# Gated cross-attention and mixture of experts: the query weights centred once, raw tokens turned, the inverse deviation as a scale of the exponentials

## The chip, the cores and the metric

One core of a Trainium2 chip runs the whole kernel. The metric is the device time in microseconds; each value is the median of several runs. A single execution is also recorded by the hardware profiler, and all rows of the profile come from that one execution. The engines are named as in the profile: PE is TensorE (PEld its weight loads), DVE is VectorE, ACT is ScalarE, POOL is GpSimd, SP is SyncE, which here only issues DMAs.

## The reference

The input `x` has 32 sequences of 128 tokens with 128 features. A second input, `ctx_512`, has 32 sequences of 128 rows with 64 features. Everything is fp32.

```
h  = layernorm(x)                        # no learned scale: (x - mean) / sqrt(var + 1e-5)
qh = (h @ Wq), kh = (ctx @ Wk), vh = (ctx @ Wv)     # 16 heads of 64
a  = softmax(qh kh^T / 8)                # per head, 128 tokens x 128 rows
x  = x + tanh(g_xattn) * ((a vh) @ Wo + bo)
h2 = layernorm(x)
x  = x + tanh(g_ffn) * (routed experts(h2) + shared expert(h2))
```

The expert part takes sigmoid scores of 32 experts in 4 groups, keeps 2 groups and then 8 experts for each token. The change does not touch it.

## The kernel before, in words

The kernel has two stages: the attention, block by block (one block `b` is one of the 32 sequences, 128 tokens), and then the experts. The first ends and the second begins at about 280 to 310 us.

**Weights folded once.** The kernel never forms keys or values. For each pair of heads it multiplies the query and key weights into one matrix (`products_a` on PE from `wqT_sb` and `wkT_sb`, and `make_a`, which copies the product to `a_sb` and multiplies it by 1/8). `make_c` does the same for values and output weights. Both work in halves of four head pairs, as there are two PSUM tiles `s_ps[0]` and `s_ps[1]`.

**One block.** `layernorm_stats` (L244, L245, DVE) gives mean and variance of a token. `inverse` adds epsilon (L299, DVE) and raises to the power -0.5 (L301, POOL) for four blocks at a time. `normalize` (L307, DVE) writes normalised tokens `xn` for two blocks. `turn_tokens` (L319, PE) transposes them and `tokens_out` (L323, ACT) copies them to `xnT`. `project` (L328, PE) multiplies by `a_sb`, `queries` (L363, ACT) copies out `qT`. `scores(b, g)` (L369, PE) multiplies one half `g` of the heads with the context `kvT_sb` into `s_ps[g]`. `negmax` (L376, DVE) takes the negated maximum of each head's row. `exponentials` (L389, ACT) runs one exponential for each of the eight heads of the half, with that maximum as a bias of one value per partition, and sums the row as it goes (the accumulator is read by a second instruction at the same line). `scaled` takes the reciprocal of the sums (L396, DVE) and multiplies the exponentials by it (L398, POOL). `turned` (L404, DVE) transposes 32 by 32 parts, `weighted` (L415, PE) multiplies with the context, `sums_out` (L424) copies the result out, half on DVE and half on ACT. `attention_out` (L436, PE) multiplies by the folded output weights, and `residual` (L442, DVE) adds the result to `x_all`, in which `add_bias` (L314, POOL) has put the output's bias.

**Order.** Everything stands in an order written out by hand (`tc.manual_schedule()`): each engine runs its own instructions in program order, and semaphores make one engine wait for another. A prelude handles blocks 0 and 1; then the loop over `b` (from L924) works on several blocks at once: in the step of `b` PE computes scores of `b` and `b+1`, the weighted sums of `b-2`, the output of `b-3` and the projection of `b+2`. Every fourth step also has logits (L487, PE; L499, ACT). From block 20 on, `gap` puts small pieces of the experts' routing between them on DVE.

**Loads.** DMAs are issued in program order on the queue of the engine that issues them. At the start ACT's queue takes the two halves of `wqT`; SP's takes `load_x(0)`, `wkT` whole, `load_x(1)`, `load_kvT(0, TB)`, `load_kv(0)`, and then the other weights. `load_rows` issues four small loads on POOL's queue.

Of the kernel before, what the change touches and what calls it, by code (L numbers as in the profile page):

```python
# [17 lines left out]
P = 128  # L18
B = 32
D = 128  # L20
KV = 64
NP = 8
TB = 4
NT = B // TB
TT = TB * P
HP = NP // 2
# [6 lines left out]
ATT_SCALE = 64.0 ** -0.5  # L33
# [21 lines left out]
def gated_cross_attention_moe(  # L55
# [22 lines left out]
    nc = tc.nc  # L78

    const = ctx.enter_context(tc.tile_pool(name="const", bufs=1))  # L80
# [3 lines left out]
    x_all = keep.tile([P, B, D], F32, tag="x", name="x_all")  # L84
# [9 lines left out]
    a2 = attn.enter_context(tc.tile_pool(name="a2", bufs=2))  # L94
    a3 = attn.enter_context(tc.tile_pool(name="a3", bufs=3))
# [31 lines left out]
    def weights(at, w):  # L127
        return x2T[:, NP * at : NP * (at + w)].rearrange("p (h c) -> p h c", h=NP)

    wqT_sb = weights(0, D)  # L130
    wkT_sb = weights(D, KV)
    wvT_sb = weights(D + KV, KV)
    wo_sb = weights(D + 2 * KV, D)
    for half in range(2):
        nc.scalar.dma_start(
            out=wqT_sb[:, half * HP : (half + 1) * HP], in_=wqT[:, half * HP : (half + 1) * HP]
        )
    load_x(0)
    nc.sync.dma_start(out=wkT_sb, in_=wkT)
    load_x(1)  # L140
    load_kvT(0, TB)
    load_kv(0)
    nc.sync.dma_start(out=wvT_sb, in_=wvT)
    nc.sync.dma_start(out=wo_sb, in_=wo)
# [42 lines left out]
    ident = const.tile([P, P], F32, tag="ident", name="ident")  # L187
# [67 lines left out]
    c_sb = aw.tile([P, NP, D], F32, tag="c", name="c_sb")  # L255

    def products_a(half):
        pa = s_ps[half].rearrange("p j q (h k) -> p j (q h) k", k=KV)
        for q in range(HP):
            for j in range(2):  # L260
                r = slice(j * KV, (j + 1) * KV)
                p = half * HP + q
                nc.tensor.matmul(
                    pa[:, j, q, :], wqT_sb[r, p, :], wkT_sb[r, p, :], start=True, stop=True
                )

    def make_a(half):
        pa = s_ps[half].rearrange("p j q (h k) -> p j (q h) k", k=KV)
        for j in range(2):
            nc.vector.tensor_scalar(  # L270
                a_sb[:, half * HP : (half + 1) * HP, j, :], pa[:, j, 0:HP, :], ATT_SCALE, None, ALU.mult
            )

    def make_c(half):
        pc = [o_ps[0][:, j].rearrange("p (h d) -> p h d", d=D) for j in range(2)]
# [15 lines left out]

    v = nc.vector
    mv1 = aw.tile([P, B, 2], F32, tag="mv1", name="mv1")
    xns, xnT, qT, nmax, es, sums, eTs, oTs = ({} for _ in range(8))
    rstds = {}

    def inverse(t):
        ve = a2.tile([P, TB], F32, tag="ve", name=f"ve_{t}")
        v.tensor_scalar(ve, mv1[:, t * TB : (t + 1) * TB, 1], EPS, None, ALU.add)  # L299
        rstds[t] = a2.tile([P, TB], F32, tag="rstd", name=f"rstd_{t}")  # L300
        nc.gpsimd.tensor_tensor(rstds[t], ve, mhalf, ALU.pow)  # L301

    def normalize(p):
        xns[p] = a2.tile([P, 2, D], F32, tag="xn", name=f"xn_{p}")
        for k in range(2):
            c = 2 * p + k
            v.tensor_scalar(  # L307
                xns[p][:, k, :], x_all[:, c, :], mv1[:, c, 0:1], rstds[c // TB][:, c % TB : c % TB + 1],
                ALU.subtract, ALU.mult,
            )  # L310

    def add_bias(p):
        a = x_all[:, 2 * p : 2 * p + 2, :]
        nc.gpsimd.tensor_tensor(a, a, tgbo.unsqueeze(1).to_broadcast([P, 2, D]), ALU.add)  # L314

    def turn_tokens(p):
        xn = xns.pop(p)
        for k in range(2):
            nc.tensor.transpose(o_ps[0][:, 1, k * P : (k + 1) * P], xn[:, k, :], ident)  # L319

    def tokens_out(p):
        xnT[p] = a3.tile([P, 2 * P], F32, tag="xnT", name=f"xnT_{p}")
        nc.scalar.copy(xnT[p], o_ps[0][:, 1, 0 : 2 * P])  # L323

    def project(b):
        x_ = xnT[b // 2][:, b % 2 * P : (b % 2 + 1) * P]
        for p in range(NP):
            nc.tensor.matmul(  # L328
                o_ps[1][:, p // HP, p % HP * P : (p % HP + 1) * P],
                a_sb[:, p].rearrange("d j k -> d (j k)"), x_, start=True, stop=True,  # L330
            )

    def first_place(k):
        return s_ps[1][:, 0, 0, :] if k else o_ps[0][:, 1, 0:P]

    def first_turned(k):

        nc.tensor.transpose(first_place(k), xns[0][:, k, :], ident)

    def first_tokens(k):  # L340
        if k == 0:
            xnT[0] = a3.tile([P, 2 * P], F32, tag="xnT", name="xnT_0")
        nc.scalar.copy(xnT[0][:, k * P : (k + 1) * P], first_place(k))

    def first_projections(b, g):

        for q in range(HP):
            nc.tensor.matmul(
                o_ps[1 - g][:, 0, q * P : (q + 1) * P],
                a_sb[:, g * HP + q].rearrange("d j k -> d (j k)"), xnT[0][:, b * P : (b + 1) * P],  # L350
                start=True, stop=True,
            )
# [21 lines left out]
    def negmax(b, g):  # L374
        nmax[b, g] = a4.tile([P, NP], F32, tag="nmax", name=f"nmax_{b}_{g}")
        v.tensor_reduce(  # L376
            nmax[b, g], s_ps[g].rearrange("p j q k -> p (j q) k"), AX.X, ALU.max, negate=True
        )

    def exponentials(b, g, js=(0, 1)):  # L380
        if (g, js[0]) == (0, 0):
            es[b] = ae.tile([P, 2, 2, HP, P], F32, tag="e", name=f"e_{b}")
        n = nmax[b, g]
        if js[0] == 0:
            sums[b, g] = a4.tile([P, NP], F32, tag="ssum", name=f"ssum_{b}_{g}")
        for j in js:
            for q in range(HP):
                c = slice(j * HP + q, j * HP + q + 1)
                nc.scalar.activation(  # L389
                    es[b][:, g, j, q, :], s_ps[g][:, j, q, :], AF.Exp,  # L390
                    bias=n[:, c], accum_out=sums[b, g][:, c],
                )

    def scaled(b, g):
# [57 lines left out]
    def clear(t):  # L452
# [7 lines left out]
        out=xs[NC * REG :, :].rearrange("(k p) w -> p k w", p=P),  # L460
        in_=zero[:, 0:RW].unsqueeze(1).to_broadcast([P, TAIL // P, RW]),
# [620 lines left out]
    xbs, wrows, wbs, wcs, own, xTs, groups, hs, hTs, ys, idx = ({} for _ in range(11))  # L1082
# [167 lines left out]
    with tc.manual_schedule():  # L1250
# [153 lines left out]
```

## Time and profile before

| | |
|---|---|
| median of 3 runs | 548.38 us (547.67 to 548.81) |
| the profiled execution, its own time | 551.0 us |
| its span, first to last instruction | 549.2 us |
| mean granted PE clock | 0.984 |
| first exponential | 16.45 us |
| start of the copy of the queries (L363), blocks 2 and 31 | 27.88 and 273.75 us |

A row of a group of instructions gives the line, the engine, the operation, output and inputs by name, shapes and count; then, after the bar, busy time in us and mean ns of one; after the next bar the idle time of the engine just before them and who ended it. A row of a wait gives who waited for whom: us in total, how often, the longest. A row of the timeline gives start, duration, engine, line, operation. Instructions of one engine overlap a little, so that a duration is longer than the time from one start to the next; both are used below, and named. A row of a stretch of time gives its length, and busy us and instructions of each engine.

### The profile page before, as it was taken

Reading aid. Unit: us, or ns where it says so; the run is one execution under the profiler, and the core shown is the slowest. Engines: PE = TensorE matmul, PEld = TensorE weight load, DVE = VectorE, ACT = ScalarE, POOL = GpSimd, SP = SyncE. Lnnn points to the kernel's source line nnn. Section 1 sums busy time; section 2 is a strip of 40 time slices with the busy share of each in tenths; the row PEclk is TensorE's granted clock in tenths of the full one; section 3 lists DMA queues with packets and bytes.
Section 4 is the critical chain, followed back from the end, with each engine's and each line's share of the span. In section 5 each row is a group of like instructions: output and inputs, shape, how many; then the busy total and the mean of one; then the engine's idle time right before and its main releaser. Section 6 shows DMA issues by size and latency. Waiting matters only on the chain.

```text
span 549.2 us, 15741 instructions
## 1 busy us (share of the span) xinstructions
PE 514.8 (94%) x5857; PEld 440.9 (80%) x5857; DVE 406.1 (74%) x920; ACT 374.5 (68%) x1407; POOL 276.8 (50%) x248
## 2 busy tenths in 40 slices
PE   5889999999999999998999789999999999999992
PEld 4777888988989988897876556666676799999992
DVE  3779999898898998998887588898644445555551
ACT  1688989989899888997883144444444677777760
POOL 5255557665675756874754641652672212232332
PEclk9899999999999999999999989999999999999997
DMA  8994440805304010000000232131123255453631
GB/s 237 236 331 144 129 174 3 300 4 175 127 20 152 3 42 1 2 2 3 2 2 26 77 94 63 35 72 15 38 49 82 56 118 122 95 131 89 128 88 15
DMA packets 49563, 47.81 MB, mean 87 GB/s; under 512 B 20752, under 2 KB 38848, under 8 KB 49104
## 3 DMA queue, kind: packets, MB, share of 16 engines
q1 hardware_dynamic: 43008, 41.71, 26.6%
q0 software_dynamic: 6192, 4.56, 5.7%
q8 instruction: 48, 0.79, 0.6%
q10 hardware_dynamic: 288, 0.52, 0.4%
q14 instruction: 27, 0.22, 0.2%
HBM read 25.44 MB, written 21.54 MB: 86 GB/s over the span
## 4 chain that ended last, share of the span: by engine, by line
PE 71%; DVE 20%; POOL 2%; ACT 2%; issue 1%; DMA 1%; another core or an unknown queue 1%; POOLq 0%; DVEq 0%
PE y L1206 11%; PE o_ps L436 8%; PE s_ps L369 8%; PE o_ps L415 7%; PE u L1190 6%; PE g L1190 6%; PE o_ps L328 6%; PE g L1124 6%; PE u L1126 5%; DVE nmax L376 5%; DVE eT L404 5%; PE ph L1144 3%; DVE xn L307 3%; DVE oT L424 1%; ACT e L389 1%
## 5 line engine op out<-in xcount | busy, mean ns | idle before, releaser
L389 ACT ACTIVATE e<-s_ps,nmax 128x128 f32<-128x128 f32 x512 | 181.6, 384 | 9.7 <-DVE nmax L376 8.3
L398 POOL TENSOR_TENSOR e<-e,rs 128x1024 f32<-128x1024 f32 x64 | 121.4, 1898 | 92.6 <-DVE rs L396 92.6
L1217 POOL DMA_INDIRECT out_dram<-o,idx x35 | 55.1, 1575 | 128.0 <-ACT o L1215 74.9
L389 ACT ACTIVATION_READ_ACCUMULATOR e<-s_ps,nmax 128x1 f32 x512 | 114.0, 223 | 0.0
L376 DVE TENSOR_REDUCE nmax<-s_ps 128x8 f32<-128x1024 f32 x64 | 77.0, 1202 | 11.7 <-PE s_ps L369 11.5
L404 DVE STREAM_TRANSPOSE eT<-e 128x1024 f32<-128x1024 f32 x64 | 78.7, 1229 | 0.9 <-POOL e L398 0.9
L369 PE MATMUL s_ps<-kvT_sb,qT 64*128 64x128 f32 x1024 | 76.0, 289 | 3.0 <-ACT e L389 1.9
L369 PEld LDWEIGHTS s_ps<-kvT_sb,qT 64*128 64x128 f32 x1024 | 63.7, 191 | 18.7 <-issue 11.1
L436 PE MATMUL o_ps<-c_sb,oT 128*128 128x128 f32 x512 | 65.4, 281 | 6.8 <-DVE oT L424 6.8
L436 PEld LDWEIGHTS o_ps<-c_sb,oT 128*128 128x128 f32 x512 | 59.7, 191 | 13.4 <-DVE oT L424 10.5
L415 PE MATMUL o_ps<-eT,kv 32*64 32x256 f32 x2048 | 66.0, 380 | 2.1 <-DVE c_sb L285 1.0
L328 PE MATMUL o_ps<-xnT,a_sb 128*128 128x128 f32 x480 | 59.9, 278 | 0.0
L1196 DVE TENSOR_TENSOR uw<-u,wb 128x512 f32<-128x512 f32 x36 | 24.9, 692 | 46.4 <-PE u L1190 41.5
L328 PEld LDWEIGHTS o_ps<-xnT,a_sb 128*128 128x128 f32 x480 | 56.7, 194 | 0.3 <-issue 0.2
L415 PEld LDWEIGHTS o_ps<-eT,kv 32*64 32x64 f32 x2048 | 49.4, 131 | 8.1 <-DVE c_sb L285 1.4
L1206 PEld LDWEIGHTS y<-ed_sb,hT 128*128 128x128 f32 x272 | 35.5, 191 | 16.0 <-issue 14.3
L698 POOL DMA_INDIRECT xs<-rows,posi x32 | 34.5, 1078 | 19.7 <-DVE nbi L727 11.0
L1131 DVE TENSOR_TENSOR uw<-u,xb 128x512 f32<-128x512 f32 x34 | 23.3, 686 | 24.2 <-PE u L1126 22.5
L1146 ACT COPY hT<-ph 128x512 f32<-128x512 f32 x34 | 19.9, 586 | 27.1 <-PE ph L1144 20.0
L1190 PE MATMUL g<-xT,wc 128*128 128x128 f32 x288 | 38.0, 275 | 0.0
L1190 PE MATMUL u<-xT,wc 128*128 128x128 f32 x288 | 38.0, 275 | 0.0
L1206 PE MATMUL y<-ed_sb,h 128*128 x288 | 37.8, 275 | 0.0
(203 smaller groups left out, 891.2 us busy)
## 6 DMA issues: line engine op xcount, KB each, us to landing
xs<-zero SPq DMA_DIRECT2D x8, 1740.0 KB, 12.2
wb<-wr SPq DMA_DIRECT2D x36, 256.0 KB, 4.0
kv<-in_kv_dram SPq DMA_DIRECT2D x32, 128.0 KB, 3.1
xb<-xs SPq DMA_DIRECT2D x35, 72.5 KB, 2.2
x_all<-in_x_dram SPq DMA_DIRECT2D x8, 256.0 KB
kvT_sb<-in_kvT_dram SPq DMA_DIRECT2D x6, 256.0 KB, 5.5
eg_sb<-in_exp_gT_dram SPq DMA_DIRECT2D x1, 1024.0 KB, 6.2
eu_sb<-in_exp_uT_dram SPq DMA_DIRECT2D x1, 1024.0 KB
```

Of the source, the lines that this page charges most:

```text
L328: nc.tensor.matmul(o_ps[1][:, p // HP, p % HP * P : (p % HP + 1) * P], a_sb[:, p].rearrange("d j k -> d (j k)"), x_, start=True, stop=True,)
L369: nc.tensor.matmul(s_ps[g][:, j, q, :], qT[b][r, g * HP + q, :], kvT_sb[r, b * P : (b + 1) * P], start=True, stop=True,)
L376: v.tensor_reduce(nmax[b, g], s_ps[g].rearrange("p j q k -> p (j q) k"), AX.X, ALU.max, negate=True)
L389: nc.scalar.activation(es[b][:, g, j, q, :], s_ps[g][:, j, q, :], AF.Exp, bias=n[:, c], accum_out=sums[b, g][:, c],)
L398: nc.gpsimd.tensor_tensor(e, e, rs.unsqueeze(2).to_broadcast([P, NP, P]), ALU.mult)
L404: v.transpose(eTs[b][:, g].rearrange("p j q n -> p (j q n)"), es[b][:, g].rearrange("p j q n -> p (j q n)"))
L415: nc.tensor.matmul(o_ps[a // 2][j * KV : (j + 1) * KV, a % 2, 0 : NP * Q].rearrange("k (g q n) -> k g q n", g=2, q=HP), kv_sb[b // TB][r, ...
L436: nc.tensor.matmul(o_ps[0][:, 0, 0:D], o[:, p].rearrange("k a n -> k (a n)"), c_sb[:, p, :], start=(p == 0), stop=(p == NP - 1),)
L698: w = nc.gpsimd.indirect_dma_start(out=xs[:, :], out_offset=bass.IndirectOffsetOnAxis(ap=posi[:, i : i + 1], axis=0), in_=rows[:, first[k] ...
L1190: nc.tensor.matmul(pt[:, q, :], w[:, k, q * P : (q + 1) * P], xTs[j], start=True, stop=True)
L1206: nc.tensor.matmul(ys[j], hT[:, q, :], ed_all[:, bass.ds(groups[j][s] * FG + q * D, D)], start=(s == 0 and q == 0), stop=(s == 1 and q == ...
L1217: w = nc.gpsimd.indirect_dma_start(out=out_rows, out_offset=bass.IndirectOffsetOnAxis(ap=idx.pop(j), axis=0), in_=o, in_offset=None, bound ...
```

## The change

- `wqT_sb` is centred in place, half by half: from each row of 128 query weights its mean is subtracted (`centre`, two DVE instructions a half). Multiplying raw tokens by centred weights is the same as multiplying centred tokens by raw weights, so the mean of a token is no longer subtracted.
- `normalize` and `xn` are gone. PE turns the raw tokens out of `x_all` (`turn_tokens`, `first_turned`); the copies are called `xT`.
- The inverse deviation of a token is applied to its scores: `exponentials` passes `deviation(b)`, one value per partition, as `scale`; `negmax` multiplies the maxima of a half by it, in place (128 partitions x 8 values, DVE). The tiles of `rstd` get three buffers instead of two.
- `make_a` is split: the first head of each pair is copied by DVE, the second by ACT.
- Loads: `wkT` comes in two halves on SP's queue, the first ahead of `load_x(0)`; `load_kvT(0, TB)` goes ahead of `load_x(1)`.
- Prelude: `load_rows` and eight transposes of the identity (`warm`) come first; then centring, the turns of blocks 0 and 1, both halves of the products; the statistics of blocks 0 to 3 come after those, and both halves of the first projections of block 0 before its scores. The statistics of blocks 4 to 8 move to the end of the prelude.

```diff
     for half in range(2):
-        nc.scalar.dma_start(
-            out=wqT_sb[:, half * HP : (half + 1) * HP], in_=wqT[:, half * HP : (half + 1) * HP]
-        )
-    load_x(0)
-    nc.sync.dma_start(out=wkT_sb, in_=wkT)
+        hs_ = slice(half * HP, (half + 1) * HP)
+        nc.scalar.dma_start(out=wqT_sb[:, hs_], in_=wqT[:, hs_])
+        nc.sync.dma_start(out=wkT_sb[:, hs_], in_=wkT[:, hs_])
+        if half == 0:
+            load_x(0)
+    load_kvT(0, TB)
     load_x(1)
-    load_kvT(0, TB)
     load_kv(0)
...
+    def centre(half):
+        hs_ = slice(half * HP, (half + 1) * HP)
+        w = wqT_sb[:, hs_, :]
+        nc.vector.tensor_reduce(mean[:, hs_], w, AX.X, ALU.add)
+        nc.vector.scalar_tensor_tensor(
+            out=w, in0=mean[:, hs_].unsqueeze(2).to_broadcast([P, HP, D]), scalar=-1.0 / D, in1=w,
+            op0=ALU.mult, op1=ALU.add,
+        )
+
+    def warm(n):
+        for _ in range(n):
+            nc.tensor.transpose(o_ps[1][:, 1, 0:P], ident, ident)
...
     def make_a(half):
         pa = s_ps[half].rearrange("p j q (h k) -> p j (q h) k", k=KV)
-        for j in range(2):
-            nc.vector.tensor_scalar(
-                a_sb[:, half * HP : (half + 1) * HP, j, :], pa[:, j, 0:HP, :], ATT_SCALE, None, ALU.mult
-            )
+        a = a_sb[:, half * HP : (half + 1) * HP]
+        w = nc.vector.tensor_scalar(a[:, :, 0, :], pa[:, 0, 0:HP, :], ATT_SCALE, None, ALU.mult)
+        tc.add_to_no_dep_group(f"a{half}", w.ins)
+        w = nc.scalar.mul(a[:, :, 1, :], pa[:, 1, 0:HP, :], ATT_SCALE)
+        tc.declare_no_dep(w.ins, group=f"a{half}", reason="each head of a pair has columns of its own")
...
-    def normalize(p):
-        xns[p] = a2.tile([P, 2, D], F32, tag="xn", name=f"xn_{p}")
-        for k in range(2):
-            c = 2 * p + k
-            v.tensor_scalar(
-                xns[p][:, k, :], x_all[:, c, :], mv1[:, c, 0:1], rstds[c // TB][:, c % TB : c % TB + 1],
-                ALU.subtract, ALU.mult,
-            )
+    def deviation(c):
+        return rstds[c // TB][:, c % TB : c % TB + 1]
...
     def turn_tokens(p):
-        xn = xns.pop(p)
         for k in range(2):
-            nc.tensor.transpose(o_ps[0][:, 1, k * P : (k + 1) * P], xn[:, k, :], ident)
+            nc.tensor.transpose(o_ps[0][:, 1, k * P : (k + 1) * P], x_all[:, 2 * p + k, :], ident)
...
+        v.tensor_scalar(nmax[b, g], nmax[b, g], deviation(b), None, ALU.mult)
...
                 nc.scalar.activation(
                     es[b][:, g, j, q, :], s_ps[g][:, j, q, :], AF.Exp,
-                    bias=n[:, c], accum_out=sums[b, g][:, c],
+                    bias=n[:, c], scale=deviation(b), accum_out=sums[b, g][:, c],
                 )
...
     with tc.manual_schedule():
-        for c in range(TB):
-            layernorm_stats(x_all, mv1, c)
-        inverse(0)
         load_rows()
-        products_a(0)
-        normalize(0)
-        make_a(0)
+        warm(8)
+        for half in range(2):
+            centre(half)
         for k in range(2):
             first_turned(k)
         for k in range(2):
             first_tokens(k)
+        products_a(0)
+        make_a(0)
+        products_a(1)
+        for c in range(TB):
+            layernorm_stats(x_all, mv1, c)
+        inverse(0)
+        make_a(1)
         first_projections(0, 0)
         first_queries(0, 0, nc.scalar.copy)
-        products_a(1)
-        for c in range(TB, 2 * TB):
-            layernorm_stats(x_all, mv1, c)
-        inverse(1)
-        make_a(1)
+        first_projections(0, 1)
+        first_queries(0, 1, v.tensor_copy)
         scores(0, 0)
         negmax(0, 0)
-        normalize(1)
-        first_projections(0, 1)
-        first_queries(0, 1, v.tensor_copy)
...
         queries(2)
-        layernorm_stats(x_all, mv1, 2 * TB)
-        normalize(2)
+        for c in range(TB, 2 * TB + 1):
+            layernorm_stats(x_all, mv1, c)
+        inverse(1)
...
-            if b % 2 == 0 and b + 4 < B:
-                normalize(b // 2 + 2)
```

More of the change, by code (lines that the diff above doesn't have):

```diff
@@ L255, in gated_cross_attention_moe @@
     c_sb = aw.tile([P, NP, D], F32, tag="c", name="c_sb")
+    mean = const.tile([P, NP], F32, tag="mean", name="mean")
+    def centre(half):
[9 more added lines that the diff above has]
+            nc.tensor.transpose(o_ps[1][:, 1, 0:P], ident, ident)
     def products_a(half):
@@ L293, in gated_cross_attention_moe @@
     mv1 = aw.tile([P, B, 2], F32, tag="mv1", name="mv1")
-    xns, xnT, qT, nmax, es, sums, eTs, oTs = ({} for _ in range(8))
+    xT, qT, nmax, es, sums, eTs, oTs = ({} for _ in range(7))
     rstds = {}
@@ L299, in inverse @@
         v.tensor_scalar(ve, mv1[:, t * TB : (t + 1) * TB, 1], EPS, None, ALU.add)
-        rstds[t] = a2.tile([P, TB], F32, tag="rstd", name=f"rstd_{t}")
+        rstds[t] = a3.tile([P, TB], F32, tag="rstd", name=f"rstd_{t}")
         nc.gpsimd.tensor_tensor(rstds[t], ve, mhalf, ALU.pow)
-    def normalize(p):
-        xns[p] = a2.tile([P, 2, D], F32, tag="xn", name=f"xn_{p}")
-        for k in range(2):
-            c = 2 * p + k
-            v.tensor_scalar(
-                xns[p][:, k, :], x_all[:, c, :], mv1[:, c, 0:1], rstds[c // TB][:, c % TB : c % TB + 1],
-                ALU.subtract, ALU.mult,
-            )
+    def deviation(c):
+        return rstds[c // TB][:, c % TB : c % TB + 1]
     def add_bias(p):
@@ L316, in turn_tokens @@
     def turn_tokens(p):
-        xn = xns.pop(p)
         for k in range(2):
-            nc.tensor.transpose(o_ps[0][:, 1, k * P : (k + 1) * P], xn[:, k, :], ident)
+            nc.tensor.transpose(o_ps[0][:, 1, k * P : (k + 1) * P], x_all[:, 2 * p + k, :], ident)
     def tokens_out(p):
-        xnT[p] = a3.tile([P, 2 * P], F32, tag="xnT", name=f"xnT_{p}")
-        nc.scalar.copy(xnT[p], o_ps[0][:, 1, 0 : 2 * P])
+        xT[p] = a3.tile([P, 2 * P], F32, tag="xT", name=f"xT_{p}")
+        nc.scalar.copy(xT[p], o_ps[0][:, 1, 0 : 2 * P])
     def project(b):
-        x_ = xnT[b // 2][:, b % 2 * P : (b % 2 + 1) * P]
+        x_ = xT[b // 2][:, b % 2 * P : (b % 2 + 1) * P]
         for p in range(NP):
@@ L336, in first_turned @@
     def first_turned(k):
-        nc.tensor.transpose(first_place(k), xns[0][:, k, :], ident)
+        nc.tensor.transpose(first_place(k), x_all[:, k, :], ident)
     def first_tokens(k):
         if k == 0:
-            xnT[0] = a3.tile([P, 2 * P], F32, tag="xnT", name="xnT_0")
-        nc.scalar.copy(xnT[0][:, k * P : (k + 1) * P], first_place(k))
+            xT[0] = a3.tile([P, 2 * P], F32, tag="xT", name="xT_0")
+        nc.scalar.copy(xT[0][:, k * P : (k + 1) * P], first_place(k))
     def first_projections(b, g):
@@ L349, in first_projections @@
                 o_ps[1 - g][:, 0, q * P : (q + 1) * P],
-                a_sb[:, g * HP + q].rearrange("d j k -> d (j k)"), xnT[0][:, b * P : (b + 1) * P],
+                a_sb[:, g * HP + q].rearrange("d j k -> d (j k)"), xT[0][:, b * P : (b + 1) * P],
                 start=True, stop=True,
```

## The prediction

> **What bounds the kernel now.** I read the page first, then the busy time of single token blocks, then the waits, then the timeline of ScalarE (ACT) and VectorE (DVE).
>
> ```profile
> span 549.2 us, 15741 instructions
> PE 514.8 (94%) x5857; PEld 440.9 (80%) x5857; DVE 406.1 (74%) x920; ACT 374.5 (68%) x1407; POOL 276.8 (50%) x248
> ...
> PE 71%; DVE 20%; POOL 2%; ACT 2%; issue 1%; DMA 1%; another core or an unknown queue 1%; POOLq 0%; DVEq 0%
> ```
>
> TensorE (PE) carries 71% of the chain, ACT 2%. ACT's 68% is an average over stages, though. The change lies in the attention, so I cut that stage at the copies of the queries (L363, one per block; starts read off the timeline):
>
> ```profile
> core 0: us, PE busy (x) PEld busy (x) DVE busy (x) ACT busy (x) POOL busy (x), PEclk, DMA share, GB/s
> 83.91:92.05 8.14, 8.14 (x132) 7.39 (x132) 7.36 (x14) 7.46 (x35) 6.24 (x6) 1.00 0.01 3
> 92.05:100.19 8.14, 8.14 (x132) 7.39 (x133) 7.75 (x15) 7.46 (x37) 6.12 (x6) 1.00 0.51 149
> 100.19:108.32 8.13, 8.13 (x132) 7.38 (x132) 6.77 (x13) 7.45 (x36) 3.79 (x3) 1.00 0.98 354
> 108.32:117.63 9.31, 9.10 (x140) 8.28 (x140) 8.38 (x17) 7.78 (x37) 6.33 (x6) 1.00 0.02 7
> ```
>
> A step is 8.14 us, PE busy throughout; each fourth step also has logits and takes 9.3. ACT is busy 7.46 of the 8.14, so it has little to give. Its only regular wait is for PE:
>
> ```profile
> ACT oT L424 <- PE o_ps L415: 17.6, 26, 0.7
> ...
> PE o_ps L436 <- DVE oT L424: 6.8, 12, 1.4
> ```
>
> That is 0.68 us a step. PE in turn loses 6.8 us in the whole loop (47 to 274 us) to DVE: all that a lighter DVE could return there.
>
> **The exponentials: the part that decides.** Each of the 512 (L389) gets a second per-partition operand, the inverse deviation as scale beside the maximum as bias; nothing is removed from ACT in the loop. The trace has an exponential with none (L499) ahead of those with one (L389), same 128x128 shape:
>
> ```profile
> 116.04 0.28 ACT L499 ACTIVATE sc<-o_ps 128x128 f32<-128x128 f32 x1
> 116.21 0.37 ACT L389 ACTIVATE e<-s_ps,nmax 128x128 f32<-128x128 f32 x1
> 116.46 0.21 ACT L389 ACTIVATION_READ_ACCUMULATOR e<-s_ps,nmax 128x1 f32 x1
> 116.55 0.38 ACT L389 ACTIVATE e<-s_ps,nmax 128x128 f32<-128x128 f32 x1
> ...
> L1215 ACT ACTIVATE o<-y,tg 128x128 f32<-128x128 f32 x35 | 12.8, 364 | 21.4 <-PE y L1206 17.6 <-PE g L1124 2.5 <-PE u L1126 1.2
> ...
> L1118 ACT COPY xT<-px 128x128 f32<-128x128 f32 x14 | 3.8, 271 | 0.0
> ```
>
> From start to start, one without an operand holds ACT for 0.17 us, one with a bias for 0.25 (116.21 to 116.46): 80 ns for one operand. A scale operand (L1215) against a plain copy (L1118) is 364 - 271 = 93 ns. No row has two. Bounds: nothing, if both are fetched together; 93 ns, if in turn. The rule is in the Trainium skill, "ScalarE: Activation LUTs", section "What ACT_TABLE_LOAD costs": each pointer operand adds about 93 ns. It speaks against this change. By the rule a step gets 16 x 93 = 1.49 us, by start-to-start 16 x 81 = 1.30. I take 87 ns, 1.39 us: the two single-operand rows agree, and one instruction fetching two at once has no row.
>
> ACT per step now, start to start: 16 x 0.343 (0.25 and 0.093 for the accumulator) = 5.49; queries 0.91; oT 0.48; tokens or turned rows 0.27; logits 0.17/4 = 0.04: 7.19. After: 7.19 + 1.39 = 8.58, above PE's 8.14. PE cannot run ahead, since `scores(b+1, 0)` needs the bank that the exponentials read. Handing over in both directions costs some 0.15 us, so ACT decides from a step of about 8.3 on, (8.3 - 7.19)/16 = 69 ns an operand. Summed over the steps between L363 starts:
> - 27.9 to 83.9: the step of b = 1 has 12 exponentials, +1.0; the six after it average 8.33, but one is 8.65 already: +1.6.
> - 83.9 to 229.1: twelve of 8.14 go to 8.58, +5.3; the long ones (9.3, 10.3) have room, 0.
> - 229.1 to 273.8: 8.47, 8.39, 8.02 go to 8.58, +0.9; 10.47 and 9.26 keep theirs.
> - Last blocks: 28 exponentials x 0.087 = 2.4, of which ACT's idle time there (0.66 + 0.19 + 0.35) hides 1.2: +1.2.
>
> Together +10.0 (with 81 ns +8, with 93 ns +12).
>
> **DVE: normalisation out, 64 small products in.** Removed: `normalize`, 32 instructions of 693 ns, 20.9 us busy, one pair per two blocks. Added: 64 products of 128x8 behind `negmax`, 0.12 to 0.17 us each by L299's small form (128x4): about 9 us. But such an instruction can wait for POOL:
>
> ```profile
> 49.40 1.90 POOL L398 TENSOR_TENSOR e<-e,rs 128x1024 f32<-128x1024 f32 x1 [0.51 <-DVE rs L396]
> 50.39 0.93 DVE L299 TENSOR_SCALAR ve<-mv 128x4 f32<-128x4 f32 x1
> ...
> 117.17 0.14 DVE L299 TENSOR_SCALAR ve<-mv 128x4 f32<-128x4 f32 x1
> ```
>
> The same instruction takes 0.14 us alone and 0.93 beside L398: it ends when POOL does. Rule: "GPSIMD Engine Reference", "Specifications", shares SBUF interfaces with VectorE and names contention with its 2-port modes. "VectorE: DVE Perf Modes", "The perf-mode tier table", gives tensor_scalar on fp32 in SBUF such a mode; the product is one. Counting by elements, 64 cost 9 us; by the row, the half-0 ones behind `scaled` meet L398 (1.90 us, started about when L376's 1.2 us does), 32 x 0.7 more = 22 us. Sum -20.9 + 9 + 22 = +10 DVE us, or 0.3 a step. That fits: in the step from 96.2 DVE idles 1.26 us. Queued behind the product are the transpose eT, on which `weighted` waits, and ACT's next exponentials, which come 4 us later. On the path: 0 now that ACT decides; a gain of up to 6.8 us if it didn't.
>
> **The start.** Before, the chain was: x landed 4.90, statistics, inverse (POOL 1.05), normalise, 16 slow products, first exponential at 16.45. After: x behind 128 KB of wk, about 5.1; centring is a reduction of 512 (half of 1.2) and an update of 512 (0.74 at L845), 1.3 a half. With wq's halves at about 3.8 and 5.3 it ends at 5.1 and 6.6. PE at its slow rate: turns 0.5, products_a 2 x 2.0, first projections 2 x 2.0 (L348 x8 at 9.38 took 2.05), scores 2.0, from 5.1: 15.6; maximum and product 1.4: exponential at 17.0, +0.5. At the full rate throughout, the same list takes half, but waits at 9.2 for a_sb's second half behind the four statistics: 12.8, -3.6. Before, PE ran from 6.3 and had its full clock only at about 16. I take it from 13: -0.7, range -3.6 to +0.6. Work hidden: `warm` (8 turns, 2 us in PE's idle first 5 us; if the identity came late, 1 us at most), make_a shared with ACT (idle), rows' DMAs earlier on POOL, one more issue on SP (0.5 us), kvT before x(1), which is read at b = 1. Stats of x(1) move behind queries(2): 5 x 0.4 us of DVE, inside b = 1's slack, at worst 1 us.
>
> **Sum.** 549.2 + 10.0 - 0.7 = 558.5 us of span. That execution's own time was 551.0, so 560.3; its sibling runs have a median of 548.38, to which the same +9.3 gives 557.7.
>
> **Rivals.**
> - Operands fetched together (ends on the other side): ACT stays at 7.19 and PE at 8.14. The start gives 0.7 to 3.6, about half of the 6.8 us wait comes back, so -5: 543. It decides below 69 ns an operand. For it: no row shows two. Against: two kinds of single operand cost the same 80 to 93 ns.
> - DVE becomes the bound: both products of a step wait 0.9 us for POOL. 2 x 1.0 - 0.8 (normalise per step) on 7.5 busy is 8.7, with waits between engines 8.9 a step; 18 normal steps x 0.3 over ACT's 8.58 is +5: 563. For it: POOL is busy 3.8 to 6.3 us of a step. Against: half-1 products come when L398 is over.
> - Nothing measurable: operand cost partly hidden, offset by the start: 548.
>
> **How the numbers follow.** Main case 0.66 (range 551 to 562, from 81/93 ns and the start's bounds), DVE bound 0.14, fetched together 0.15, nothing 0.05. About 0.2% is what can be told from no change. Slower 0.80, same 0.05, faster 0.15. The range runs from 547, which takes in the unchanged case, to 567, half-way beyond the DVE case; it leaves out the faster case and a tail.
>
> **What would show it.** Right: exponentials some 90 ns longer and 0.43 from start to start; L363 starts 8.5 to 8.7 apart; the ACT wait for PE (0.68) gone and PE waiting for ACT's exponentials in its place; the small product at 0.13 or near 0.8 by what POOL does; first exponential near 15.7. Wrong: exponentials still 0.343 apart, or a clock that is full before 10 us, or DVE without idle time in a step.

## The result, and the profile after

The changed kernel takes 571.8 us (median of 4 runs, 571.68 to 572.44) against 548.48 us (a fourth run of before added to the three above): 1.043 times as long, interval 1.0412 to 1.0448. The forecast was 557.7: the direction holds, but the loss is 23.3 us instead of 9.3. The profiled execution of after took 571.86 us, that of before 551.0, so the two traces differ by 20.9 us; before's profiled execution stood 2.6 us above the median of its siblings, after's on it.

From the page of after (span; busy time; shares of the chain), and from its groups of instructions the row of the exponentials, whose mean was 384 ns without the second operand, and the row of the new products:

```profile
span 570.1 us, 15806 instructions
PE 530.4 (93%) x5865; PEld 441.0 (77%) x5865; DVE 414.3 (73%) x954; ACT 418.5 (73%) x1409; POOL 275.0 (48%) x248
...
PE 53%; ACT 31%; DVE 10%; DMA 2%; issue 2%; POOL 0%; SPq 0%; POOLq 0%; DVEq 0%; ACTq 0%
...
L402 ACT ACTIVATE e<-s_ps,nmax,rstd 128x128 f32<-128x128 f32 x512 | 229.9, 487 | 6.7 <-DVE nmax L391 5.1 <-DVE rs L409 0.6 <-DVE eT L417 0.5
...
L391 DVE TENSOR_SCALAR nmax<-nmax,rstd 128x8 f32<-128x8 f32 x64 | 22.9, 358 | 2.3
```

ACT's share of the chain goes from 2% to 31%. ACT is still busy only 73% of the span, so the average says nothing about what binds; the step does. Cut at the copies of the queries (now L375), four steps in a row from the copy of block 9 on, as in the cut of before, read:

```profile
core 0: us, PE busy (x) PEld busy (x) DVE busy (x) ACT busy (x) POOL busy (x), PEclk, DMA share, GB/s
90.93:100.06 9.13, 8.71 (x134) 7.30 (x130) 7.89 (x16) 8.83 (x37) 6.39 (x6) 1.00 0.01 2
100.06:109.20 9.14, 8.72 (x134) 7.30 (x130) 7.73 (x15) 8.84 (x38) 6.05 (x6) 1.00 0.57 147
109.20:118.33 9.13, 8.71 (x134) 7.30 (x130) 7.12 (x15) 8.83 (x37) 3.79 (x3) 1.00 0.85 305
118.33:127.74 9.41, 8.99 (x132) 7.64 (x130) 7.82 (x16) 9.11 (x38) 5.79 (x5) 1.00 0.01 3
```

A normal step takes 9.13 us where it took 8.14; the forecast was 8.58. PE is no longer busy throughout (8.71 of 9.13), and ACT isn't either (8.83 of 9.13). So neither engine's total sets the step. The waits between 50 and 280 us show both of them waiting for each other (total us, how often, longest):

```profile
PEld o_ps L428 <- ACT qT L375: 18.1, 25, 0.9
...
PEld s_ps L381 <- ACT e L402: 9.6, 25, 0.4
...
PE o_ps L428 <- ACT qT L375: 7.9, 20, 0.4
ACT oT L437 <- PE o_ps L428: 7.5, 25, 0.3
```

The new one is that `weighted` (PE, L428) waits for the copy of the queries. The timeline shows how it goes on from there, in one step (a selection of its rows):

```profile
100.06 1.08 ACT L375 COPY qT<-o_ps 128x1024 f32<-128x1024 f32 x1
100.11 0.66 PE L428 MATMUL o_ps<-eT,kv 32*64 32x256 f32 x8
100.96 0.55 ACT L402 ACTIVATE e<-s_ps,nmax,rstd 128x128 f32<-128x128 f32 x1
...
101.19 1.96 PE L428 MATMUL o_ps<-eT,kv 32*64 32x256 f32 x56 [0.42 <-ACT qT L375]
...
102.27 0.55 ACT L402 ACTIVATE e<-s_ps,nmax,rstd 128x128 f32<-128x128 f32 x1
...
103.22 0.59 ACT L437 COPY oT<-o_ps 128x512 f32<-128x512 f32 x1 [0.30 <-PE o_ps L428]
103.70 0.46 ACT L402 ACTIVATE e<-s_ps,nmax,rstd 128x128 f32<-128x128 f32 x1
```

`queries` reads the PSUM tile `o_ps[1]`. `weighted` writes half of its results to that tile, so after eight matmuls it stands until ACT has copied the queries, and then needs 1.96 us more. ACT has only four exponentials to fill that time (100.96 to 102.71); then it waits for `weighted`, since its next instruction in program order is the copy of oT out of the same tile. That is a closed loop through one bank: from the start of the queries' copy to that of oT 3.16 us; the copy of oT 0.48; eight exponentials; the tokens 0.25; four more exponentials of the next block; and the next copy of the queries. With exponentials 0.436 us apart this is 3.16 + 0.48 + 0.25 + 12 x 0.436 = 9.12, the measured step. The four exponentials inside the 3.16 cost nothing; the other twelve all count. Whether this loop is what binds is tested below by runs that lengthen it, lengthen only what lies outside it, and open it.

By place, from the starts of the queries' copies of blocks 2 and 31:

| | before | after | measured | forecast |
|---|---|---|---|---|
| up to block 2 | 27.88 | 29.28 | +1.4 | -0.7 |
| block 2 to 31 | 245.9 | 265.8 | +19.9 | +8.8 |
| block 31 to the end | 275.5 | 275.1 | -0.4 | +1.2 |
| span | 549.2 | 570.1 | +20.9 | +9.3 |

Only the middle row can be read to a few tenths of a us: two other kernels below with the steps of before take 245.8 and 246.1 there. The first and the last row scatter from execution to execution by some 3 us. Near the end, the granted clock stood at 0.50 for 6.8 us in before (313.4 to 316.8 and 327.1 to 330.5) and in after (345.7 to 352.6), for 3.4 in the run with four operands and not at all in the run without warm-up turns, whose last row reads 272.1. What repeats there is the way from the queries' copy of block 31 to the last exponential: 13.1 us in before and in the run with four operands, 14.8 in after and in the run without warm-up turns, so +1.7. With the 1.4 us that the new start alone costs in its runs below, 19.9 + 1.7 + 1.4 = 23.0 of the 23.3 us are placed.

### The profile page after: what moved, and what is told of

Its sections match the earlier page's. It is cut to its first block, busy times and chain, and to the rows that moved or that the text cites. A ratio compares the mean times of both kernels' runs of the same rounds, so it can differ in the third digit from the quotient of the medians.

```text
span 570.1 us, 15806 instructions
## 1 busy us (share of the span) xinstructions
PE 530.4 (93%) x5865; PEld 441.0 (77%) x5865; DVE 414.3 (73%) x954; ACT 418.5 (73%) x1409; POOL 275.0 (48%) x248
## 3 DMA queue, kind: packets, MB, share of 16 engines
q1 hardware_dynamic: 43152, 41.71, 26.7%
## 4 chain that ended last, share of the span: by engine, by line
PE 53%; ACT 31%; DVE 10%; DMA 2%; issue 2%; POOL 0%; SPq 0%; POOLq 0%; DVEq 0%; ACTq 0%
ACT e L402 23%; PE y L1216 10%; PE o_ps L428 9%; PE g L1134 5%; PE u L1136 5%; PE u L1200 5%; PE g L1200 5%; ACT qT L375 4%; PE ph L1154 3%; ACT oT L437 2%; DVE nmax L388 2%; DVE eT L417 2%; PE o_ps L449 2%; PE s_ps L381 1%; DVE nmax L391 1%
## 5 line engine op out<-in xcount | busy, mean ns | idle before, releaser
L402 ACT ACTIVATE e<-s_ps,nmax,rstd 128x128 f32<-128x128 f32 x512 | 229.9, 487 | 6.7 <-DVE nmax L391 5.1
L402 ACT ACTIVATION_READ_ACCUMULATOR e<-s_ps,nmax,rstd 128x1 f32 x512 | 119.5, 233 | 0.0
L428 PE MATMUL o_ps<-eT,kv 32*64 32x256 f32 x2048 | 80.2, 383 | 11.5 <-ACT qT L375 9.1
L428 PEld LDWEIGHTS o_ps<-eT,kv 32*64 32x64 f32 x2048 | 47.5, 131 | 33.7 <-ACT qT L375 20.6
L340 PE MATMUL o_ps<-xT,a_sb 128*128 128x128 f32 x480 | 60.1, 279 | 0.0
L340 PEld LDWEIGHTS o_ps<-xT,a_sb 128*128 128x128 f32 x480 | 57.0, 195 | 0.3 <-issue 0.2
L1216 PEld LDWEIGHTS y<-ed_sb,hT 128*128 128x128 f32 x272 | 35.6, 192 | 15.3 <-issue 15.3
L711 POOL DMA_INDIRECT xs<-rows,posi x32 | 33.6, 1050 | 20.1 <-DVE nbi L740 11.4
L1141 DVE TENSOR_TENSOR uw<-u,xb 128x512 f32<-128x512 f32 x34 | 23.3, 686 | 24.7 <-PE u L1136 24.6
L1156 ACT COPY hT<-ph 128x512 f32<-128x512 f32 x34 | 19.9, 586 | 26.1 <-PE ph L1154 25.1
```

The costliest lines, as they stand in the source:

```text
L340: nc.tensor.matmul(o_ps[1][:, p // HP, p % HP * P : (p % HP + 1) * P], a_sb[:, p].rearrange("d j k -> d (j k)"), x_, start=True, stop=True,)
L402: nc.scalar.activation(es[b][:, g, j, q, :], s_ps[g][:, j, q, :], AF.Exp, bias=n[:, c], scale=deviation(b), accum_out=sums[b, g][:, c],)
L428: nc.tensor.matmul(o_ps[a // 2][j * KV : (j + 1) * KV, a % 2, 0 : NP * Q].rearrange("k (g q n) -> k g q n", g=2, q=HP), kv_sb[b // TB][r, ...
L711: w = nc.gpsimd.indirect_dma_start(out=xs[:, :], out_offset=bass.IndirectOffsetOnAxis(ap=posi[:, i : i + 1], axis=0), in_=rows[:, first[k] ...
L1216: nc.tensor.matmul(ys[j], hT[:, q, :], ed_all[:, bass.ds(groups[j][s] * FG + q * D, D)], start=(s == 0 and q == 0), stop=(s == 1 and q == ...
```

## The experiments

Two theories stood at the start. A: the second operand on ACT is the whole loss. B: the product on DVE, or rather what is queued behind it, is a good part of it. A third question was what the new start brings.

A warning first for the expectations of the runs that touch the start: they speak of a start that is 2.3 us earlier. That was a misreading of after's trace, with a wrong zero of time. The right figures are a first exponential at 16.99 us against 16.45, and the queries' copy of block 2 at 29.28 against 27.88.

**The operand taken away.** After without the scale (so the scaling of the scores is left out of this kernel and of the one under "The product moved", which builds on it):

```diff
-                    bias=n[:, c], scale=deviation(b), accum_out=sums[b, g][:, c],
+                    bias=n[:, c], accum_out=sums[b, g][:, c],
```

> The changed kernel without the scale operand of the exponentials (the scores' multiplication by the inverse deviation is left out there; the maxima are still multiplied). Theory A, that the second per-partition operand of each exponential holds ACT about 93 ns longer and that this, with a wait it brings, is the whole loss: exponentials again 0.343 us from start to start, steps about 8.1, and the earlier start (2.3 us) stays, so 543 to 547 us. Theory B, that the small products behind the maxima on DVE (with their waits for POOL) cost the time: still above 560 us. Theory C, that the raw tokens, the loads or the new order of the prelude cost it: still above 565 us.

Measured: 555.17 us, 1.0129 times before (1.0108 to 1.0150); the trace is that of the fastest of the four runs (551.47 to 556.3). Most of the loss is gone, but block 2 to 31 still takes 252.5 us, 6.6 more than before. Theory A, with the whole loss in the operand, falls.

**The operand alone.** Before with a column of ones as scale, nothing else:

```diff
-                    bias=n[:, c], accum_out=sums[b, g][:, c],
+                    bias=n[:, c], scale=ones[:, 0:1], accum_out=sums[b, g][:, c],
```

> The kernel before with one thing added: the exponentials get a column of ones as scale operand, so the values are the same. Theory A: ACT's exponentials go from 0.343 to 0.436 us apart and the steps from 8.14 to about 9.1 us as in the changed kernel, so 548.4 + 20 in the loop + 3 in the last blocks = 571 us (568 to 575). Theories B and C: 548 us, since neither the products nor the prelude nor the loads are there.

Measured: 570.49 us, 1.0399 (1.0381 to 1.0416); block 2 to 31 takes 265.6 us, within 0.2 of after, in steps of 9.12. So the operand alone is enough for after's loop, although taking it away doesn't give everything back: the two causes don't add, each is a bound, and the slower one shows.

**The product alone.** Before with the maxima multiplied by ones on DVE:

```diff
             nmax[b, g], s_ps[g].rearrange("p j q k -> p (j q) k"), AX.X, ALU.max, negate=True
         )
+        v.tensor_scalar(nmax[b, g], nmax[b, g], ones[:, 0:1], None, ALU.mult)
```

> The kernel before with one other thing added: each half's maxima are multiplied by a column of ones on DVE, in place, before the exponentials use them; normalisation stays. Theory A: DVE has 0.4 to 1.3 us of idle time in a step and the exponentials use the maxima late, so 548 to 552 us. Theory B: 560 us or more. In either case the products take about 0.23 us alone and 0.8 to 0.95 where POOL's multiplication of the exponentials is running.

Measured: 565.95 us, 1.0333 (1.0281 to 1.0385); block 2 to 31 takes 263.8 us, +17.9. That is far above what I gave it: 64 instructions of 0.23 us of work each cost some 17 us. The timeline shows one way in which they do it:

```profile
100.05 1.90 POOL L399 TENSOR_TENSOR e<-e,rs 128x1024 f32<-128x1024 f32 x1 [1.40 <-DVE rs L397]
...
101.13 0.84 DVE L379 TENSOR_SCALAR nmax<-nmax,ones 128x8 f32<-128x8 f32 x1
101.89 1.23 DVE L405 STREAM_TRANSPOSE eT<-e 128x1024 f32<-128x1024 f32 x1
```

The product ends with POOL's instruction (100.05 + 1.90 = 101.95), and the transpose eT comes behind it. ACT waits for that transpose, because the tile of exponentials has two buffers: the next block's first exponential writes the one that eT reads last. That is not the whole of it. The waits of ACT between 50 and 275 us:

```profile
ACT e L390 <- DVE nmax L379: 6.7, 13, 1.4
ACT e L390 <- DVE eT L405: 6.5, 12, 0.6
```

Before had 2.3 us of waits for the maxima and no such wait for eT, and PE's waits for DVE's copy of oT rose from 6.4 to 10.8 us. So ACT waits as long for the product itself as for the transpose behind it, and the rest reaches PE through the copy of oT. Here DVE's order still has the normalisation that after dropped; without it, in the first experiment, the loop was 6.6 us longer than that of before.

**The product moved.** The kernel of the first experiment, with the half-0 product put behind that transpose in DVE's order:

```diff
-        v.tensor_scalar(nmax[b, g], nmax[b, g], deviation(b), None, ALU.mult)
+        if g or b < 2:
+            product(b, g)
...
             turned(b - 1, 1)
+            if b + 1 < B:
+                product(b + 1, 0)
             scaled(b, 1)
```

> The changed kernel without the scale operand (left out as in the run without it, which took 551 to 556 us), with the half-0 product moved behind the transpose of the exponentials on DVE, where POOL's multiplication is over. If the loss left there is the product waiting for POOL with the transpose queued behind it, and ACT's next exponentials waiting for the buffer that the transpose frees: the products fall to about 0.23 us each and the time to 545 to 549 us. If the products cost by their number alone: 552 to 556 us again.

Measured: 544.85 us, 0.993 (0.9893 to 0.9967), 10.3 us below the first experiment; block 2 to 31 takes 243.0 us, and normal steps 8.14 again. The waits of ACT between 50 and 280 us, first without the operand:

```profile
ACT oT L437 <- PE o_ps L428: 17.5, 26, 0.7
...
ACT e L402 <- DVE eT L417: 4.7, 12, 0.6
```

and with the product moved (the wait for eT is not among them any more):

```profile
ACT oT L441 <- PE o_ps L432: 18.3, 27, 0.7
```

So the 6.6 us that stayed behind came from the product's place ahead of the transpose, not from the number of products: all 64 are still there (17.0 us of DVE's time instead of 26.2, as fewer of them run beside POOL). The loop is now even 2.9 us shorter than that of before, which still has the normalisation on DVE. The same move in the kernel with the operand was not tried; the loop through the bank stands above it there.

**Which exponentials count.** The loop through the bank says that twelve of a block's sixteen count, and ACT's total says that all do. Before with the ones operand in four only, those between the queries' copy and oT's:

```diff
-                    bias=n[:, c], accum_out=sums[b, g][:, c],
+                    bias=n[:, c], scale=ones[:, 0:1] if (g, j) == (0, 1) else 1.0, accum_out=sums[b, g][:, c],
```

> Before, with the ones operand in four exponentials of a block alone, those between the copy of the queries and the copy of oT. Loop theory: they lie inside the time that ACT waits for the weighted values anyway (0.9 + 4 x 0.436 = 2.64 of 3.16 us), so the step stays at 8.14: 548 to 549 us. If any 93 ns on ACT costs by itself, 512/4 = 128 operands x 0.093 = 11.9 us would come: 560 us.

Measured: 548.06 us, 1.000 (0.9986 to 1.0015). 128 operands, 11.9 us of ACT's time, cost nothing; they come out of ACT's wait for `weighted`. Between 50 and 280 us it was, in before and then here:

```profile
ACT oT L424 <- PE o_ps L415: 18.3, 27, 0.7
...
ACT oT L424 <- PE o_ps L415: 8.5, 27, 0.3
```

The other way round, in half 1's eight:

```diff
-                    bias=n[:, c], accum_out=sums[b, g][:, c],
+                    bias=n[:, c], scale=ones[:, 0:1] if g else 1.0, accum_out=sums[b, g][:, c],
```

> Before, with a column of ones as scale operand in half 1's eight exponentials of a block alone (nothing else changed). Two readings of the loss remain. Loop theory: the step is set by a loop through PSUM bank 1, queries copied, weighted values, oT copied, twelve exponentials (half 1's eight and half 0's last four of the next block), tokens, queries; it takes 7.90 us before, and these eight operands lengthen it by 8 x 0.093 = 0.74 to 8.64, above PE's 8.14: some 18 normal steps x 0.5 = +9, 557 us. Total theory (ACT's work of a step against PE's): 7.19 + 0.74 = 7.93 is below 8.14, so nothing: 548 to 549 us.

Measured: 562.19 us, 1.028 (1.0243 to 1.0318). ACT's total of 7.93 us lies below PE's 8.14, and still a step takes 8.77 us, of which ACT is busy 8.10 (same columns as above):

```profile
95.24:104.01 8.77, 8.71 (x136) 7.30 (x134) 7.76 (x15) 8.10 (x38) 6.11 (x6) 1.00 0.54 162
...
104.01:112.77 8.76, 8.71 (x135) 7.29 (x133) 6.66 (x13) 8.09 (x37) 3.79 (x3) 1.00 0.85 308
```

ACT's total as the bound falls; the loop holds. I had it at 7.90 us without operands and so expected 8.64 and 557 us. Eight operands give 8.76 and twelve 9.13, 93 ns each; carried back to none, the loop is 8.02 us (an estimate). So before had 0.12 us of slack in it, 10 ns for each of twelve exponentials. Its timeline shows that slack as the gap ahead of the queries' copy: the last exponential starts at 99.71, the next ACT instruction would be due 0.34 us later, at 100.05, and the copy starts at 100.19.

**Queries copied earlier.** After with the queries' copy ahead of the last two of the four exponentials, so that `weighted` starts earlier:

```diff
-                exponentials(b + 1, 0, (0,))
+                exponentials(b + 1, 0, (0,), (0, 1))
             if b + 2 < B:
                 queries(b + 2)
+            if b + 1 < B:
+                exponentials(b + 1, 0, (0,), (2, 3))
```

> The changed kernel with one change of order on ACT: the copy of the queries goes ahead of the last two of the four exponentials that stood before it, so six exponentials instead of four stand between that copy and the copy of the weighted sums. Theory A with the bank: PE's weighted sums write the bank that the copy of the queries reads, take 2.0 us after it, and ACT has only four exponentials (1.74 us) to fill that; with six (2.6 us) the wait at the weighted sums (about 0.4 us a step) goes, steps fall from 9.13 to 8.65 - 8.75, and the time to 558 - 562 us. If instead the whole extra step is the exponentials' own time, nothing changes: 571 us.

Measured: 565.83 us, 1.0309 (1.0291 to 1.0327), above the 558 to 562 expected; steps of 8.90. ACT's wait for `weighted` is gone, but it now waits for the projection that it copies (0.29 us in a normal step: the last exponential starts at 105.94, and 0.436 later the copy is due, which starts at 106.67), and PE waits for the later exponentials. The waits between 50 and 280 us:

```profile
PE s_ps L381 <- ACT e L402: 17.4, 25, 0.7
...
ACT qT L375 <- PE o_ps L340: 2.2, 5, 0.4
```

That is a second loop: from the queries' copy over six exponentials to the scores 3.71 us (97.77 to 101.48), and from the scores over the output and the projection to the next copy 5.19 (to 106.67), together 8.90.

With only one exponential passed by:

```diff
-                exponentials(b + 1, 0, (0,))
+                exponentials(b + 1, 0, (0,), (0, 1, 2))
             if b + 2 < B:
                 queries(b + 2)
+            if b + 1 < B:
+                exponentials(b + 1, 0, (0,), (3,))
```

> The changed kernel with the copy of the queries one exponential earlier (three before it, one after) instead of two. Two earlier gave steps of 8.90 us, with ACT waiting 0.29 us for the projection at that copy. Loop through the bank (oT copy 0.48, eleven exponentials at 0.436, tokens 0.25, queries 0.90, weighted sums 2.1 with hand-overs): 8.6 us; ACT's own sum 8.62. Steps of 8.65 to 8.75, 560 to 562 us, if the bank and the projection are the two waits and the rest is ACT's own time; 566 us again if something else holds the step.

Measured: 564.04 us, 1.0281 (1.0244 to 1.0318), above the 560 to 562 expected; normal steps of 8.64 to 8.72, block 2 to 31 in 257.8 us. Here ACT waits for neither, and its total, 0.90 + 0.48 + 0.25 + 16 x 0.436 = 8.61, is the step to within 0.1. This is the step that I had forecast; it comes only once the loop is opened. Both runs moved in the expected direction, by less than expected, and neither came back to before.

**The new start alone.** After's loads, centring and prelude, with operand and product for blocks 0 and 1 only, and the old normalised loop behind it:

```diff
+        if b < 2:
+            v.tensor_scalar(nmax[b, g], nmax[b, g], deviation(b), None, ALU.mult)
...
-                    bias=n[:, c], accum_out=sums[b, g][:, c],
+                    bias=n[:, c], scale=deviation(b) if b < 2 else 1.0, accum_out=sums[b, g][:, c],
...
+        normalize(1)
+        for c in range(TB, 2 * TB):
+            layernorm_stats(x_all, mv1, c)
+        inverse(1)
         scores(1, 0)
```

> The changed kernel's loads, centring, prelude and raw tokens for blocks 0 and 1 (with scale operand and products for these two blocks alone); from block 2 on tokens are normalised on DVE as before, without operand and products. The start alone gave 2.3 us (with operands) to 3 us (without) by block 4 in the runs so far and the loop is the old one: 545 to 546.5 us. If the start's gain is made good again by waits later in the loop: 548 us.

Measured: 550.39 us (20 runs), 1.0025 (1.0009 to 1.0041), against the 545 to 546.5 that rested on the misread start. The new start brings no gain but a loss of 1.4 us (0.5 to 2.3); block 2's queries are copied at 28.42 us against 27.88, and block 2 to 31 takes 246.1.

**No warm-up turns.** After without `warm(8)`:

```diff
         load_rows()
-        warm(8)
```

> The changed kernel without its eight warm-up turns. If they bring PE's full clock earlier, the first exponential comes up to 2 us later than 16.99: 572 to 574 us. If they do nothing: 571 to 572 us.

Measured: 571.27 us, 1.0444 (1.0416 to 1.0471), after's ratio of 1.043 within the interval; its profiled execution has the first exponential at 16.59 us. The eight turns do nothing that these runs can tell. In after's start, PE does the first 16 projections at half rate (3.78 us; the 16 of a later step take 1.95), gets its full rate at 14.6 us, and loses it again after a wait (timeline, PE alone):

```profile
9.82 3.78 PE L360 MATMUL o_ps<-xT,a_sb 128*128 128x128 f32 x16
...
20.67 1.38 PE L381 MATMUL s_ps<-kvT_sb,qT 64*128 64x128 f32 x16 [2.20 <-ACT e L402]
...
24.19 2.08 PE L381 MATMUL s_ps<-kvT_sb,qT 64*128 64x128 f32 x16 [1.52 <-ACT e L402]
26.20 3.04 PE L340 MATMUL o_ps<-xT,a_sb 128*128 128x128 f32 x16
```

The granted clock was 0.50 from 21.5 to 28.3 us here and from 23.3 to 26.7 in before: 3.4 us more of half rate. At the measured rates, 3.4 us at half clock are about 1.7 us of work lost, which is more than the 1.4 by which block 2 starts later. The other traces bear this out. With before's start, the queries' copy of block 2 stood at 26.33 and 26.63 us in the two executions that had no half rate before it (the product alone; half 1's operand), at 27.88 to 28.36 in three that had 3.4 us of it (before, four operands, the old start normalised on POOL), and at 29.31 with 3.4 us of it and the operand in all exponentials. With the new start, seven of eight traces had 6.8 us of it and stood at 28.42 to 29.77; the eighth, the operand taken away, had none and stood at 25.64. So without the half rate the new start may well be the earlier one; that rests on one execution. That the waits of PE in the new start bring the longer spell is argued, as no run held them fixed.

**Normalisation on POOL.** If DVE's order is a cost in the loop, the normalisation can leave it without any operand on ACT: the kernel of "The new start alone", with the blocks from 2 on normalised by GpSimd:

```diff
-            v.tensor_scalar(
+            nc.gpsimd.tensor_scalar(
```

> The kernel with the new start and the old loop, but the normalisation of blocks 2 to 31 on POOL instead of DVE. PE's waits for DVE's copy of the weighted sums (6.8 us in the old loop) should shrink, if POOL, busy 6.2 of 8.1 us of a step, finds room for 0.8 us a step: 542 to 544 us. If POOL's multiplication of the exponentials comes late behind it: 548 us or more.

Measured: 546.7 us (20 runs), 0.9958 (0.9939 to 0.9976), not the 542 to 544 expected; block 2 to 31 takes 241.7 us, 4.2 less than in before. The same move in before with its own start, for the pairs from the third on:

```diff
-            v.tensor_scalar(
+            (nc.gpsimd if p > 1 else v).tensor_scalar(
```

> Before, with the normalisation of all token pairs from the third block on moved from VectorE to GpSimd, and the start as it was. The loop lost 4.2 us where the same was done behind the new start (546.7 against 550.4); with the old start it should give 548.5 - 4 = 544 to 545 us, if the new start's 1 to 2 us are lost for good. If the start makes no difference: 546 to 547.

Measured: 546.62 us (20 runs), 0.9969 (0.9956 to 0.9982). Both are faster than before, by 0.3 to 0.4%, and so than after. The second missed its 544 to 545: block 2 to 31 takes 243.1 us instead of 241.7, because one step takes 12.0 us (10.4 in the first), and 2.2 us of that are a wait. In the timeline POOL, which had been kept busy, is late with the exponentials' multiplication; the transpose waits for it, the copy of oT is behind the transpose, and PE waits:

```profile
233.16 3.75 POOL L398 TENSOR_TENSOR e<-e,rs 128x1024 f32<-128x1024 f32 x2
...
235.09 1.25 DVE L404 STREAM_TRANSPOSE eT<-e 128x1024 f32<-128x1024 f32 x1 [2.31 <-POOL e L398]
...
239.51 3.68 PE L436 MATMUL o_ps<-c_sb,oT 128*128 128x128 f32 x16 [2.17 <-DVE oT L424]
```

## Why the prediction was right and wrong

- **The operand's price: right.** I took 87 ns between 80 and 93, and a rival had the two operands fetched together. Exponentials are 0.436 us apart (before 0.343), so a second operand costs 93 ns, what the Trainium skill states for each ("ScalarE: Activation LUTs", section "What ACT_TABLE_LOAD costs"); the busy mean went from 384 to 487. The 6 ns are 0.1 us a step and not the miss. The rival at 543 falls with the operand alone at 570.49.
- **"The ACT wait for PE (0.68) gone", "ACT decides from a step of about 8.3 on, 69 ns an operand": the step that failed.** I set ACT's total against PE's total. The total was well worked out: 8.58 forecast, 8.61 from after's timeline. But the wait stays at 0.52 us (from the end of the fourth exponential, 102.71 by the spacing, to 103.22; by the same count it was 0.81 in before), because it isn't slack of ACT: it is part of a loop through `o_ps[1]`, in which ACT is held by `weighted` and `weighted` by ACT's own copy of the queries before it. 8.61 + 0.52 = 9.13. The row that I quoted, ACT waiting 0.68 us in 26 of the steps, was the loop's mark; I read it as spare time. The threshold was 10 ns on each of twelve exponentials, not 69 on sixteen; the 0.15 us that I allowed for handing over is not at fault, as before's trace shows hand-overs of 0.04 (projection to queries' copy) and 0.08 us (`weighted` to the copy of oT). The loop's term of the sum was +8.8 and measured +19.9; the runs with four and with eight operands show it to be this loop.
- **DVE's products: size too high, place wrong.** Forecast 9 + 22 us of busy time, measured 22.9: 0.23 us alone where I had 0.12 to 0.17, and 13 of the 64 at 0.5 to 0.95 where I had 32. That DVE's total rose by 8.2 us where I had +10 is luck: normalisation and products together made some +2, and the rest came from work that this sum left out (4.4 us from the small additions of epsilon, which grew longer, and 2.7 from the centring). That the path cost is 0 "now that ACT decides" holds in after: with the operand alone the loop is as long. But "a gain of up to 6.8 us if it didn't" is wrong in sign: without the operand the loop loses 6.6 us, through the transpose that I had named as queued behind the product and then not priced. With the product out of its way the gain exists: 2.9 us in the loop, and 4.2 where only the normalisation leaves DVE. I looked at when the exponentials need the maxima (4 us later), and not at when their buffer comes free.
- **The rival "DVE becomes the bound", 563:** its two products of 0.9 us weren't there, and DVE's busy time is not the limit in after (7.89 of 9.13 us at most in the normal steps shown). What exists is DVE's order, with one late transpose, and in after it is hidden behind the loop through the bank.
- **The start: -0.7 forecast, +1.4 measured** up to block 2, and +1.4 in the runs of the new start alone. The first exponential came at 16.99, the figure (17.0) of the list at PE's slow rate, which I had worked out and then averaged with the fast one. The range given for the term ended at +0.6; it had no place for the half-rate spell that follows the start, 6.8 us in after and 3.4 in before.
- **Last blocks: +1.2 forecast, +1.7 measured.** From the queries' copy of block 31 to the last exponential after takes 14.8 us (295.04 to 309.82), before 13.1 (273.74 to 286.85). The -0.4 of the table takes in the experts' part behind it, which the change doesn't touch and which scatters: 262.4 us in before's execution, 260.3 in after's, 259.1 in that with four operands, 257.4 in that without warm-up turns.
- **The range** (547 to 567) was built from prices of the operand and of the product. No bound in it asked what happens if the wait I took as ACT's reserve isn't one: +0.5 us on each of some 20 normal steps is 10 of the 11.1 us by which the loop's term fell short.

## What to carry to other kernels

An engine's wait that recurs in every step, with the same length, isn't spare time until it has been followed round: if the engine that it waits for was itself waiting for this engine's previous instruction, through the same buffer or bank, the two form a loop, and only the work between its two ends is free. Add up that loop and set it against the step, beside the engines' totals. Price a small instruction by what stands behind it in its engine's order and by when that frees a buffer, rather than by its own length.

## What was not expected of the hardware

- A product of 128x8 takes 0.23 us alone, and 0.84 (up to 0.95) when POOL is in a long elementwise instruction: it ends when POOL's does. 64 of them, about 15 us of work if each is alone, lengthened the kernel before by some 17 us.
- A wait of PE can be paid twice. In the step of 12.0 us above, the granted clock after the 2.17 us wait was 0.51 and 0.50 in the two stretches that follow, and 16 matmuls took 3.68 us where they otherwise take 2.05:

```profile
core 0: us, PE busy (x) PEld busy (x) DVE busy (x) ACT busy (x) POOL busy (x), PEclk, DMA share, GB/s
236.20:239.60 3.40, 1.23 (x21) 1.04 (x17) 3.30 (x17) 1.84 (x8) 0.71 (x1) 1.00 0.00 0
239.60:241.50 1.90, 1.90 (x9) 1.90 (x10) 1.90 (x2) 1.65 (x10) 1.86 (x1) 0.51 0.00 0
241.50:243.00 1.50, 1.50 (x9) 1.50 (x9) 0.39 (x2) 0.00 (x0) 1.07 (x2) 0.50 0.00 0
```

- POOL took 816 ns for the normalisation of a block (128x128) that DVE did in 693, so that giving POOL 28 of the 32 added 20.1 us to POOL's busy time (276.8 to 296.9) and took 15.3 off DVE's (406.1 to 390.8), and the kernel got shorter.
